# A two-layer graph network on one core: layer two's first block held by chunks of inputs, one block's rows moved in the DMA queue, and the last superblocks' weight sums read from PSUM

## The chip, the cores and the metric

The kernel runs on one core of a Trainium2 chip, in one launch. The metric is the device time of that launch in microseconds; three runs of the kernel before give its median. Beside the runs there is one profiled execution, from which all views of the trace come: PE (TensorE, the matmuls), PEld (its weight loads), DVE (VectorE), ACT (ScalarE), POOL (GpSimd) and SP (SyncE, which here only issues DMAs).

## What is computed

`x` is 128 × 64 × 768 (batches, positions, features), `adj` 128 × 64 × 64. All is float32. Cut to what matters:

```python
h = maximum(layernorm(x), 0)
for l in range(2):
    m_left  = einsum('bsh,oh->bso', h, W_left[l])
    m_right = einsum('bsh,oh->bso', h, W_right[l])
    u_left  = einsum('bih,bjh->bij', h, m_left) / sqrt(768)
    u_right = einsum('bih,bjh->bij', h, m_right) / sqrt(768)
    u = u_left on and above the diagonal of adj, u_right below it
    attention = exp(u) * adj, normalised over j
    h_lin = einsum('bsh,oh->bso', h, W_lin[l]) + b_lin[l]
    ctx = attention @ h_lin
    h = relu((ctx - mean) / (std + eps) * ln_a[l] + ln_b[l])
out = x + h
```

The two score products and the linear map are matrix products of 8192 tokens with 768 × 768 weights.

## The kernel before

**Parts, blocks, superblocks.** The 8192 tokens are 16 blocks of 512 (T), or 32 parts of 256 (TH), 4 batches each. `HT` holds a part's inputs transposed: features on the partitions, six chunks (C) of 128, as a tile `ht` of [128, 6, 256]. `SUPER` (L173) groups the parts that are worked on together: first the two parts (0, 1), then eleven superblocks of three parts.

**Pass one** (`pass_one`, L655) makes scores and attention. The products of tokens with W_left and W_right go by a fast bilinear scheme: three groups of tokens against blocks of 256 × 256 of the weights, in 40 products (`PRODUCTS`) instead of 54. Each product multiplies a signed sum of weight blocks (a "form", `W_OPS`) with a signed sum of token blocks (`T_OPS`, made by class `Tokens`, mostly on POOL); six of the 40 use a raw token block, index below 9. `product` (L691) issues eight matmul instructions of 256 columns (a float32 matmul appears as two instructions), the result lies in one of six PSUM banks (C, D, X, Y, Z, V, taken in turn), and `reads` (L904) adds it with its coefficients into the score operands M: the first touch of each by an ACT copy (L910), the others by DVE (L245, the helper `added`, and L914). A product must wait until its bank was read. Behind a superblock come its scores (L733) and softmax.

**The first block of layer two** is different. Layer two's k = 0 covers one block of 512 tokens. The three groups are thirds of each batch's 64 positions, 22 wide (`WIDE`, `THIRDS`, L579 to L581), so a product has 8 × 22 = 176 columns. The block lies in two `ht` tiles, one for each part (four batches, six chunks). A raw token block therefore is two pieces of 88 columns, one in each tile, and its product takes 16 instructions instead of 8; sums that read a raw block are made in two halves of 176 elements (`value(..., cut=True)`). Weight forms of layer two were made in layer one and lie in DRAM; 20 are fetched ahead (`forms_first`, L1328), the others during k = 0, each into a buffer that came free (`fetch`, L936 to L937 and in `turn_of`).

**Pass two** (`pass_two`, L1012) takes one block after another: h_lin (`linear`, L1226, 15 products of `ORDER`, L1006), context (L1048), and the normalisation in `finish` (L1182): squares (L1193) into a buffer `z` (a ring of four), then the scaled rows (L1211), which are stored (`kept`, L1180). In the last two blocks of layer one (u = 14 and 15) layer two is prepared: rows of blocks 0 and 1 are loaded (`load_rows`, L344, eight DMAs), transposed by DVE into `xb`, stored (L461, four DMAs), and loaded again transposed (`load_h`, L370, two DMAs of 768 KB), where the affine map and relu are applied by ACT (`affine`, L383, L379).

**What sets the order.** All is written out in program order. A product or multiplication i opens slots 2i and 2i + 1; `put(slot, f)` hangs a step on a slot, `run` issues it there, and each engine works through its own instructions in that order. All transfers here are issued by SP through one queue, in order: a DMA that waits holds those behind it. The lines around the change:

```python
1271  put(27, lambda: load_rows(1, 1, sp))           # in the loop, u = 14
1289  load_h(1, 1, 0)                                # start of u = 15
1290  put_all(24, transpose_rows(1, 1, sp), 2)
1293  put(48, lambda: load_h(1, 1, 1))
1294  put_all(28, affine(1, 1, 0), 3)
```

**The last superblock of each layer** also prepares the linear weights of pass two (`final_of`, L1310): they are loaded, centred by ACT with sums and differences (`centre`, L218, L233 and L237, slots 28 on), and 16 signed sums of them are made (`sums_n`, L247), the even ones on POOL, the odd ones on DVE, from slot 42 on, two in every three slots. `bias` (L955) treats the bias rows likewise; its `combined` (L978) adds three of them on DVE (L979, L980).

Of the kernel before, what the change touches and what calls it, by code (L numbers as in the profile page):

```python
# [17 lines left out]
def kernel(  # L18
# [12 lines left out]
    nc = tc.nc  # L31
# [549 lines left out]
    CUT = PB * WIDE  # L581

    class Tokens:
# [11 lines left out]
        def value(self, k, v, cut=False):  # L595
            if v >= 9:
                t = self.at[k, v]
                if k:
                    return [t]
                t = t[:, :, :2 * CUT]  # L600
                return [t[:, :, h * CUT:(h + 1) * CUT].rearrange("p c (b s) -> p c b s", b=PB)
                        for h in range(2)] if cut else [t]
            j = v // 3
            if k:
                return [HT[1, self.l, SUPER[k][v % 3]][:, j * K2:(j + 1) * K2, :]]
            r = THIRDS[v % 3][0]
            return [HT[1, self.l, p][:, j * K2:(j + 1) * K2, :].rearrange("p c (b s) -> p c b s", s=S)[:, :, :, r:r + WIDE]
                    for p in SUPER[0]]
# [7 lines left out]
        def emit(self, eng):  # L616
# [4 lines left out]
            cut = a < 9 or b < 9  # L621
            for o, x, y in zip(*(self.value(self.k, n, cut) for n in (v, a, b))):
# [12 lines left out]
        def need(self, k, v):  # L635
            while v >= 9 and (k, v) not in self.at:
                self.emit(nc.gpsimd)
            return self.value(k, v)
# [16 lines left out]
    def pass_one(l, start, final):  # L655
        with tc.tile_pool(name=f"one{l}", bufs=2, reuse_waits="tile") as sp, \
# [34 lines left out]
            def product(bank, w, ts, new, slot, n=TH):  # L691
                p = bank[:, :2 * n].rearrange("p (g n) -> p g n", g=2)
                for g in range(2):
                    for c in range(K2):
                        at = 0
                        for t in ts:
                            t = t[:, c]
                            n = math.prod(t.shape[1:])
                            o = p[:, g, at:at + n]
                            if len(t.shape) == 3:  # L700
                                o = o.rearrange("p (b s) -> p b s", b=t.shape[1])
                            nc.tensor.matmul(o, w[:, c, g * P:(g + 1) * P], t,  # L702
                                             start=(new and g == c == at == 0), stop=(c == K2 - 1),
                                             skip_group_check=True)
                            at += n
# [659 lines left out]
```

## Time and profile before

| | us |
|---|---|
| median of three runs | 2652.43 (2652.22 to 2653.41) |
| the profiled execution | 2648.42 |
| its span, first to last instruction | 2646.6 |
| PE busy | 2591.6 (98%) |
| DVE busy | 1780.6 (67%) |
| POOL busy | 1763.1 (67%) |
| ACT busy | 935.4 (35%) |

The mean granted TensorE clock was 0.995 of full speed. A line of the timeline gives start, duration, engine, source line, operation, what is written and read, and the count; in brackets stands the idle time of the engine before it and what ended it. In the lists of DMA issues the last number is the time from issue to landing. Where the profile names one releaser, an instruction may have waited for several things, of which it names the one that it saw last.

### The profile page before, as it was taken

How to read it: one execution, taken by the hardware profiler on the slowest of the kernel's cores; microseconds unless marked ns; L12 is line 12 of the kernel's file. 1: busy time of each engine (PE TensorE's matmuls, PEld its weight loads, DVE VectorE, ACT ScalarE, POOL GpSimd, SP SyncE). 2: the span in 40 equal slices, each digit the busy share in tenths (PEclk: the TensorE clock that was granted, in tenths of full speed). 3: DMA queues.
4: the chain of work that ended last, by engine and by line, in shares of the span. 5: the costliest groups of instructions: out<-in, count | busy, mean ns of one | idle time of the engine just before them, and what ended most of it. 6: DMA issues, size and time to landing. Idle time of an engine off the chain costs nothing. (4 is left out here: it accounts for less than half of the span.)

```text
span 2646.6 us, 47202 instructions
## 1 busy us (share of the span) xinstructions
PE 2591.6 (98%) x18122; PEld 2217.1 (84%) x18122; DVE 1780.6 (67%) x2888; ACT 935.4 (35%) x1969; POOL 1763.1 (67%) x1392
## 2 busy tenths in 40 slices
PE   9899999999999999999999999999999989999998
PEld 8788888888888888888798888888888878887886
DVE  7878787777768445554456667677666676666667
ACT  5522223223113244454542222122222335555453
POOL 4766676666668657676276666667666657878786
PEclk9999999999999999999999999999999999999999
DMA  7443534343421354445794424253532215555655
GB/s 220 113 111 86 124 93 110 93 119 79 98 60 56 123 156 149 159 139 182 219 282 101 121 68 108 71 129 93 136 98 70 67 49 157 157 167 166 177 161 146
DMA packets 258465, 331.84 MB, mean 125 GB/s; under 512 B 56002, under 2 KB 190402, under 8 KB 258242
## 3 DMA queue, kind: packets, MB, share of 16 engines
q1 hardware_dynamic: 241442, 320.56, 44.3%
q10 hardware_dynamic: 16800, 8.26, 1.2%
q8 instruction: 145, 2.38, 0.4%
q14 instruction: 78, 0.64, 0.1%
HBM read 213.39 MB, written 115.34 MB: 124 GB/s over the span
## 5 line engine op out<-in xcount | busy, mean ns | idle before, releaser
L245 POOL TENSOR_TENSOR g<-ht 128x512 f32<-128x512 f32 (+1 forms) x620 | 785.9, 1279 | 420.8 <-PE Z L702 71.6
L245 POOL TENSOR_TENSOR g<-g,g 128x512 f32<-128x512 f32 (+1 forms) x310 | 397.9, 1291 | 136.7 <-PE C L702 22.0
L245 POOL TENSOR_TENSOR g<-ht,g 128x512 f32<-128x512 f32 (+1 forms) x272 | 346.1, 1282 | 164.8 <-PE Z L702 42.8
L702 PE MATMUL X<-g,g 128*128 128x256 f32 (+1 forms) x1080 | 252.9, 377 | 6.0 <-DVE m L914 6.0
L1006 PE MATMUL Z<-g,g 128*128 128x256 f32 x1024 | 244.1, 380 | 3.5 <-ACT hl L300 3.2
L702 PE MATMUL C<-g,g 128*128 128x256 f32 x1008 | 239.7, 381 | 4.9 <-POOL g L245 2.2
L702 PEld LDWEIGHTS X<-g,g 128*128 128x128 f32 x1080 | 203.0, 191 | 34.8 <-DVE m L914 6.8
L702 PE MATMUL Y<-g,g 128*128 128x256 f32 (+1 forms) x968 | 225.7, 376 | 3.8 <-POOL g L245 3.8
L1006 PEld LDWEIGHTS Z<-g,g 128*128 128x128 f32 x1024 | 191.6, 190 | 35.8 <-issue 4.1
L379 ACT ACTIVATE ht<-ht,b_col,a_col 128x256 f32<-128x256 f32 x384 | 196.1, 591 | 69.0 <-DMA ht<-h 53.8
L702 PEld LDWEIGHTS C<-g,g 128*128 128x128 f32 x1008 | 190.5, 190 | 32.9 <-POOL g L245 3.5
L702 PE MATMUL Z<-g,g 128*128 128x256 f32 (+1 forms) x936 | 217.0, 375 | 0.0
L702 PE MATMUL D<-g,g 128*128 128x256 f32 x880 | 209.8, 381 | 1.8 <-POOL g L245 1.8
L702 PEld LDWEIGHTS Y<-g,g 128*128 128x128 f32 x968 | 182.0, 190 | 27.8 <-POOL g L245 4.2
L702 PE MATMUL V<-g,g 128*128 128x256 f32 (+1 forms) x840 | 194.6, 375 | 3.1 <-POOL g L245 1.6
L702 PEld LDWEIGHTS Z<-g,g 128*128 128x128 f32 x936 | 174.5, 190 | 23.1
L702 PEld LDWEIGHTS D<-g,g 128*128 128x128 f32 x880 | 168.1, 191 | 25.7 <-POOL g L245 2.5
L1006 PE MATMUL X<-g,g 128*128 128x256 f32 x768 | 182.7, 379 | 0.0
L702 PEld LDWEIGHTS V<-g,g 128*128 128x128 f32 x840 | 157.6, 191 | 23.3 <-POOL g L245 1.7
L1206 POOL TENSOR_TENSOR z<-z,b 128x768 f32<-128x768 f32 x62 | 112.7, 1829 | 81.7 <-DVE z L1203 77.2
L245 DVE TENSOR_TENSOR m<-m,Y 128x512 f32<-128x512 f32 (+2 forms) x196 | 126.5, 667 | 58.4 <-ACT m L910 35.7
L245 DVE TENSOR_TENSOR m<-m,D 128x512 f32<-128x512 f32 x180 | 118.2, 677 | 70.0 <-ACT m L910 51.3
(222 smaller groups left out, 4612.0 us busy)
## 6 DMA issues: line engine op xcount, KB each, us to landing
ht<-h SPq DMA_DIRECT2D x126, 768.0 KB, 6.3
h<-xb SPq DMA_DIRECT2D x124, 384.0 KB, 6.6
z<-z SPq DMA_DIRECT2D x128, 192.0 KB, 3.1
x<-z SPq DMA_DIRECT2D x128, 192.0 KB, 5.4
xr<-in_x_dram SPq DMA_DIRECT2D x120, 192.0 KB, 3.8
out_dram<-xr SPq DMA_DIRECT2D x120, 192.0 KB, 2.7
x<-in_x_dram SPq DMA_DIRECT2D x112, 192.0 KB, 5.4
g<-form SPq DMA_DIRECT2D x40, 256.0 KB, 5.6
```

The costliest lines, as they stand in the source:

```text
L245: (eng.tensor_add if sign == "+" else eng.tensor_sub)(o, a, b)
L379: nc.scalar.activation(ht, ht, AF.Relu, bias=cols[1][:, c:c + 1], scale=cols[0][:, c:c + 1])
L702: nc.tensor.matmul(o, w[:, c, g * P:(g + 1) * P], t, start=(new and g == c == at == 0), stop=(c == K2 - 1), skip_group_check=True)
L1006: nc.tensor.matmul(p[:, n], b[t][:, c, r * P:(r + 1) * P], w[s][:, c, :], start=(i in FIRST and i not in PRELOAD and n == c == 0), stop=(c ...
L1206: nc.gpsimd.tensor_add(zs[k], zs[k], rows["b"])
```

## The change

It has three parts.

1. **First block of layer two.** Its 512 tokens are held as two `ht` tiles of three chunks and all tokens, instead of two of six chunks and half the tokens. `load_both` fills them by four DMAs of 384 KB (pieces of 1 KB in each partition) in place of two of 768 KB. A raw token block lies in one tile, or, for the middle pair of chunks, one chunk in each. Raw products take eight instructions of 176 columns instead of 16 of 88. Token sums that read raw blocks are one operation of 352 elements, save where a middle block is read: these stay two, by chunk. The affine map takes six ACT operations of 512 elements instead of twelve of 256.
2. **Second block of layer two.** Its row loads move from slot 27 of u = 14 to slot 1 of u = 15, behind the first block's loads; the transposes from slots 24 to 36 to slots 32 to 44 and their store from 40 to 48; the loads of the transposed block from slot 48 to 54, behind the stores of z from u = 15's first half (slots 51 and 52).
3. **Last superblock of each layer.** For the eight odd sums, and for both additions in `combined`, ACT first copies one operand into PSUM (bank Z or V in turn), and DVE reads it there.

The diff, cut to its core:

```diff
@@ sums_n
-            added((nc.gpsimd, nc.vector)[n % 2], t[o], s, t[a], t[b])
+            x = t[a]
+            if n % 2:
+                x = KEEP["ZV"[n // 2 % 2]].rearrange("p (c d) -> p c d", c=K2)
+                nc.scalar.copy(x, t[a])
+            added((nc.gpsimd, nc.vector)[n % 2], t[o], s, x, t[b])
...
+    CUT = 2 * PB * WIDE
+
+    def load_both(l):
+        for n in range(2):
+            t = HT[1, l, n] = big.tile([P, C, TH], F32, name="ht", bufs=6).rearrange("p c t -> p (c t)").rearrange(
+                "p (c t) -> p c t", t=T)
+            for p in range(2):
+                nc.sync.dma_start(t[:, :, p * TH:(p + 1) * TH], KEPT[l][p][:, n * C // 2:(n + 1) * C // 2])
+
+    def both_of(l, c, n):
+        return HT[1, l, 2 * c // C][:, c % (C // 2):c % (C // 2) + n]
+
+    def affine_both(l):
+        def part(c):
+            t = both_of(l, c, 1)[:, 0]
+            nc.scalar.activation(t, t, AF.Relu, bias=cols[1][:, c:c + 1], scale=cols[0][:, c:c + 1])
+
+        return [lambda c=c: part(c) for c in range(C)]
...
@@ Tokens.emit
-            cut = a < 9 or b < 9
-            for o, x, y in zip(*(self.value(self.k, n, cut) for n in (v, a, b))):
+            if self.k == 0 and (a // 3 == 1 or b // 3 == 1):
+                for c in range(K2):
+                    added(eng, *([self.value(0, v, c), sign] + [self.value(0, n, c) for n in (a, b)]))
+            else:
+                o, x, y = (self.value(self.k, n) for n in (v, a, b))
...
                 added(eng, o, sign, x, y)
@@ product
-                        at = 0
-                        for t in ts:
-                            t = t[:, c]
-                            n = math.prod(t.shape[1:])
-                            o = p[:, g, at:at + n]
...
+                        t = tok(c)
+                        o = p[:, g] if len(t.shape) == 2 else p[:, g].rearrange("p (b s) -> p b s", s=WIDE)
+                        nc.tensor.matmul(o, w[:, c, g * P:(g + 1) * P], t, start=(new and g == c == 0),
+                                         stop=(c == K2 - 1), skip_group_check=True)
@@ combined
-            nc.vector.tensor_add(t[1], t[1], t[0])
-            nc.vector.tensor_add(t[3], t[1], t[2])
+            a, b = (KEEP[n][:, :D] for n in "ZV")
+            nc.scalar.copy(a, t[0])
+            nc.scalar.copy(b, t[2])
+            nc.vector.tensor_add(t[1], t[1], a)
+            nc.vector.tensor_add(t[3], t[1], b)
@@ pass_two, u = 14
-                        put(27, lambda: load_rows(1, 1, sp))
@@ pass_two, u = 15
-                        load_h(1, 1, 0)
-                        put_all(24, transpose_rows(1, 1, sp), 2)
+                        load_both(1)
+                        put(1, lambda: load_rows(1, 1, sp))
+                        put(31, lambda: put_all(32, transpose_rows(1, 1, sp), 2))
                         put_all(2, [fetch.popleft() for _ in range(8)], 2)
                         put_all(46, [lambda: TOKENS[1].step(0)] * Tokens.LIMIT, 1)
-                        put(48, lambda: load_h(1, 1, 1))
-                        put_all(28, affine(1, 1, 0), 3)
+                        put(54, lambda: load_h(1, 1, 1))
+                        put_all(28, affine_both(1), 3)
```

More of the change, by code (lines that the diff above doesn't have):

```diff
@@ L592, in __init__, with value @@
             self.count = {}
-        def value(self, k, v, cut=False):
+        def value(self, k, v, c=None):
+            if k:
+                t = self.at[k, v] if v >= 9 else HT[1, self.l, SUPER[k][v % 3]][:, v // 3 * K2:(v // 3 + 1) * K2, :]
+                return t if c is None else t[:, c, :]
             if v >= 9:
[L597 to L608, printed above, removed]
+                t = self.at[k, v][:, :, :CUT]
+                return t if c is None else t[:, c].rearrange("p (b s) -> p b s", s=WIDE)
+            n, r = v // 3 * K2 + (c or 0), THIRDS[v % 3][0]
+            t = both_of(self.l, n, K2 if c is None else 1).rearrange("p c (b s) -> p c b s", s=S)[:, :, :, r:r + WIDE]
+            return t if c is None else t[:, 0]
         def step(self, slot, eng=None):
@@ L689, in pass_one, with product @@
                 "p (k h) -> p k h", k=2) for g in range(2)]
-            def product(bank, w, ts, new, slot, n=TH):
+            def product(bank, w, tok, new, slot, n=TH):
                 p = bank[:, :2 * n].rearrange("p (g n) -> p g n", g=2)
@@ L729, in scores @@
                             b = q % 2 * PAIR + h
-                            mb = both[:, c, q // 2 * PB + b] if l and k == 0 else m[:, c, b]
+                            if l and k == 0:
+                                b += q // 2 * PB
+                                hc, mb = both_of(l, c, 1)[:, 0], both[:, c, b]
+                            else:
+                                hc, mb = ht[:, c], m[:, c, b]
                             mb = mb.rearrange("p k j -> p (k j)")
@@ L882, in pass_one @@
                     tok = HT[1, l, t][:, j * K2:(j + 1) * K2, :]
-                    product(bank, weights.at[3 * w + j], [tok], j == 0, slot)
+                    product(bank, weights.at[3 * w + j], lambda c, tok=tok: tok[:, c, :], j == 0, slot)
                     weights.used(3 * w + j)
@@ L919, in pass_one @@
                     w, tok = weights.need(f), tokens.need(k, t)
-                    product(bank_of(CHAINS * (k - 1) + i % CHAINS), w, tok, i < CHAINS, slot, TH if k else 2 * CUT)
+                    product(bank_of(CHAINS * (k - 1) + i % CHAINS), w, tok, i < CHAINS, slot, TH if k else CUT)
                     tokens.used(k, t)
```

15 lines of the change are left out of this document (5 added, 10 removed).

## The prediction

> **What bounds the kernel now.** I read the page first, its share of each engine, then the busy time by stretches, and then the timeline of the stretches that the diff touches.
>
> ```profile
> PE 2591.6 (98%) x18122; PEld 2217.1 (84%) x18122; DVE 1780.6 (67%) x2888; ACT 935.4 (35%) x1969; POOL 1763.1 (67%) x1392
> 820.00:864.00 44.00, 39.20 (x300) 33.08 (x299) 38.79 (x57) 12.19 (x38) 34.62 (x27) 1.00 0.04 11
> 1297.00:1336.00 39.00, 35.87 (x189) 25.02 (x188) 15.40 (x36) 24.68 (x56) 8.04 (x16) 1.00 1.00 307
> 1336.00:1392.50 56.50, 53.44 (x369) 52.84 (x368) 31.67 (x66) 22.37 (x49) 40.92 (x60) 0.97 0.93 271
> 1392.50:2088.00 695.50, 690.74 (x5672) 609.05 (x5674) 477.62 (x779) 171.44 (x331) 460.71 (x368) 1.00 0.39 96
> ```
>
> The page gives TensorE 98% of the span, so time is won only by fewer or shorter matmuls, or where PE waits. The stretches (columns: length, then PE, weight loads, DVE, ACT, POOL, then clock, DMA share, GB/s) show where that is: 820 to 864 is layer one's last superblock, with DVE at 38.8 of 44; 1297 to 1336 is the last block of layer one's second pass and 1336 to 1392.5 is layer two's first block, and in both the DMA engines are all but full (1.00 and 0.93). Behind that, from 1392.5 on, PE works 690.7 of 695.5: little there can hand back or swallow what happens ahead of it.
>
> PE's waits in these stretches, from the timeline (start, duration, idle before and its releaser):
>
> ```profile
> 837.23 1.99 PE L702 MATMUL X<-g,g 128*128 128x256 f32 x8 [2.90 <-DVE m L914]
> 848.62 1.97 PE L702 MATMUL C<-g,g 128*128 128x256 f32 x8 [0.58 <-DVE m L245]
> 1317.60 1.13 PE L1006 MATMUL Z<-g,g 128*128 128x256 f32 x4 [1.68 <-ACT hl L300]
> 1320.41 1.13 PE L1006 MATMUL Z<-g,ht 128*128 128x256 f32 x4 [0.81 <-ACT hl L300]
> 1327.06 1.13 PE L1006 MATMUL Z<-g,ht 128*128 128x256 f32 x4 [0.47 <-ACT hl L300]
> 1391.15 1.43 PE L702 MATMUL V<-g,g 128*128 128x176 f32 x8 [1.47 <-DVE m L914]
> 2137.22 3.38 PE L702 MATMUL X<-g,g 128*128 128x256 f32 x8 [3.10 <-DVE m L914]
> ```
>
> The profiled execution took 2648.42 us, of which 1.8 lie outside its span of 2646.6. The median of the three runs is 2652.43, 4.0 above it. I make the sum as a difference in the profiled execution and add it to the median.
>
> **Part one, layer two's first block.** Its six products of raw tokens lose half their matmuls.
>
> ```profile
> 1359.47 1.36 PE L702 MATMUL X<-g,g 128*128 128x176 f32 x8
> 1360.66 1.91 PE L702 MATMUL Y<-ht,g 128*128 128x88 f32 x16
> 1362.41 1.39 PE L702 MATMUL Z<-g,g 128*128 128x176 f32 x8
> 1384.90 0.36 SPq L651 DMA_DIRECT2D g<-form  x1
> g<-form SPq DMA_DIRECT2D x1, 256.0 KB, 6.1
> ```
>
> From start to start a raw product (16 instructions of 88) costs 1362.41 − 1360.66 = 1.75 us, a summed one (8 of 176) 1360.66 − 1359.47 = 1.19. Six products save 6 × 0.56 = 3.4 us of PE. But the last product of this block, at 1391.15, needs the last weight form, which SP issues at 1384.90 and which lands 6.1 us later (the last row, an answer on DMA issues at that moment): at 1391.0. The DVE that the profile names is not what came last. So a PE that arrives 3.4 us earlier waits 3.4 us longer, unless the form comes earlier too. **The DMA queue decides here**, and it is one queue in order, nearly full: the form comes earlier only by what is gained or lost in gaps of the transfers ahead of it.
>
> ```profile
> 1334.52 0.93 SPq L368 DMA_DIRECT2D ht<-h  x1
> ht<-h SPq DMA_DIRECT2D x1, 768.0 KB, 6.6
> 1345.33 0.60 ACT L379 ACTIVATE ht<-ht,b_col,a_col 128x256 f32<-128x256 f32 x1 [1.11 <-DMA ht<-h]
> DMA packets 344, 1.08 MB, mean 362 GB/s; under 512 B 59, under 2 KB 59, under 8 KB 344
> DMA packets 3050, 2.94 MB, mean 367 GB/s; under 512 B 180, under 2 KB 3050, under 8 KB 3050
> 1294.54 1.99 SPq L461 DMA_DIRECT2D h<-xb  x1
> h<-xb SPq DMA_DIRECT2D x1, 384.0 KB, 7.9
> ```
>
> - A gap that goes. Today the second load of the other block waits for a store: the first load lands at 1334.52 + 6.6 = 1341.1, the second at 1345.3 (ACT starts on it then). 768 KB at 362 GB/s (the row of 1342 to 1345 us) is 2.2 us, so 4.2 − 2.2 = 2.0 us are empty. In the new order four z stores (192 KB each, 2.2 us by the same rate) stand ahead of these loads and fill the gap: −1.9.
> - A gap that comes. The new loads go to the head of the last block, and the second needs the last transposed store, which lands at 1294.54 + 7.9 = 1302.4. Today rows stream behind that store without a break. A load needs about 2 us from its issue to its first bytes, by the empty 2.0 just found, and the first quarter (384 KB, 1.1 us at 367 GB/s) needs only an earlier store and covers part: +0.8.
> - The pieces. 4 loads of 384 KB in 1-KB pieces replace 2 of 768 KB. The row with 3050 packets (8 to 16 us: weights in 1-KB pieces, 256 KB each) shows 367 GB/s: 4 × 1.07 = 4.3 against 2 × 2.2 = 4.4 us: −0.1. The Trainium skill (DMA: Bandwidth & Descriptors, Rules for kernel authors) speaks against this edit: it asks for 1 MiB or more in a DMA. By that the halved loads would move slower and the form would land later; the two rows, 362 and 367 GB/s, do not bear it out.
>
> Sum for the form: −1.9 + 0.8 − 0.1 = −1.2, ends −2.1 (no new gap) and +1.2 (the old gap not filled, a new one of 1.2). The PE needs 3.4 and gets 1.2.
>
> The token sums and the affine step are cheaper, and I cost them at nothing:
>
> ```profile
> L245 POOL TENSOR_TENSOR g<-ht 128x176 f32<-128x176 f32 x33 | 16.6, 535 | 0.0
> L245 POOL TENSOR_TENSOR g<-g,g 128x352 f32<-128x352 f32 x12 | 11.2, 937 | 0.5
> ```
>
> Two sums of 176 (2 × 0.54, or about 1.0 pitch to pitch) become one of 352 (0.94): about 0.1 each, under 2 us in all, on an engine busy 40.9 of 56.5. Without this cover the loss is at most the same 2 us.
>
> **Part two, the second block's rows behind the stores.** What SP does now at the end of layer one, and why ACT holds PE there:
>
> ```profile
> 1296.57 6.88 SPq L361 DMA_DIRECT2D x<-z  x8
> 1306.90 1.19 SPq L1180 DMA_DIRECT2D z<-z  x2
> z<-z SPq DMA_DIRECT2D x2, 192.0 KB, 7.6
> 1315.07 0.81 ACT L1193 ACTIVATE z<-aux 128x768 f32<-128x768 f32 x1 [2.73 <-PE Z L1006]
> 1324.53 0.81 ACT L1193 ACTIVATE z<-aux 128x768 f32<-128x768 f32 x1 [0.25 <-DMA z<-z]
> ```
>
> The squares at 1315.07 write a z buffer that the stores of 1306.90 must first empty; they land 7.6 us later, at about 1315.0. PE had long been done. ACT stands 2.73 us, and PE's evictions stand behind it: 1.68 + 0.81 = 2.5 us of the waits listed. Those stores are late because eight row loads (6.9 us) went ahead. With the rows behind, the stores land some 5 us earlier (6.9 less the new gap and the loads' pieces) and this wait goes: −2.5. What is late next: the squares at 1324.53, which today wait 0.25 for the next z stores. Ahead of those the queue carries as much as before, the rows now among it, plus the new gap of 0.8: they land 0.8 later, while PE and ACT get there 2.5 earlier. So ACT stands there instead, and the wait before 1327.06 (0.47) grows by about 2.7. Net +0.2, between −2.5 (nothing late) and +0.8. It hardly matters for the end, since the form at 1391 is set by the queue: what PE gains here it waits for there.
>
> The four transposes move by 8 slots with their store (40 to 48), and the second block's loads by 6 (48 to 54), past the z stores. SP waits for the store before the second load, as today; behind it on SP stand z stores and the next rows, which the full queue would hold anyway. I cost this at nothing; what it costs without that cover is the slower rival.
>
> **Part three, the staged weight sums.** Per layer eight copies of 512 and two of 256 come onto ACT; DVE's sums read PSUM.
>
> ```profile
> L245 DVE TENSOR_TENSOR g<-g,g 128x512 f32<-128x512 f32 x8 | 10.0, 1246 | 0.0
> L245 DVE TENSOR_TENSOR m<-m,Y 128x512 f32<-128x512 f32 x11 | 7.0, 675 | 0.0
> L979 DVE TENSOR_TENSOR g<-g 128x256 f32<-128x256 f32 x1 | 1.5, 1480 | 0.0
> L980 DVE TENSOR_TENSOR g<-g,g 128x256 f32<-128x256 f32 x1 | 1.4, 1369 | 0.0
> 821.15 0.68 DVE L245 TENSOR_TENSOR g<-g,g 128x512 f32<-128x512 f32 x1
> 824.65 0.40 ACT L233 ACTIVATE g<-g 128x256 f32<-128x256 f32 x1
> 825.57 0.16 DVE L228 TENSOR_REDUCE wmm<-wm 128x2 f32<-128x6 f32 x1 [1.66 <-ACT g L233]
> 831.39 0.69 DVE L245 TENSOR_TENSOR m<-m,D 128x512 f32<-128x512 f32 x1 [1.17 <-ACT m L910]
> 851.12 0.59 ACT L995 COPY Z<-g 128x512 f32<-128x512 f32 x1
> ```
>
> With PSUM as one operand a sum of 512 takes 0.675, so eight go from 10.0 to 5.4; L979 and L980, of 256, from 2.9 to at most 1.35 (two at the price of 512): DVE is relieved of 4.6 + 1.5 = 6.1 us a layer. The Trainium skill (SBUF — State Buffer, Who interferes with whom) says why: a DVE instruction with two SBUF inputs contends with a GpSimd one that reads SBUF, one with a single SBUF input doesn't. The rows agree (1.25 in the mean against 0.675).
>
> But the copies queue on ACT behind the centring of the weights, in slot order. DVE reaches the first odd sum at 821.15; the copy for it (slot 43) stands just ahead of the centring step of slot 44, which ACT starts at 824.65. With 0.59 for the copy (the last row) DVE gets its operand at 825.3, 4.1 us late. Of that, 1.66 and 1.17 us are waits that DVE has today (at 825.57 and 831.39), but the first one's release comes from ACT, whose next steps wait for DVE's L229 in turn, so that ACT falls back by about 2 and by another 1.2 for two more copies. At 831.39 DVE is then about 2.7 late. From there to the wait at 837.23 one sum and L979, L980 give back about 1.1 + 1.5 = 2.6, and the next copies (0.59 and two smaller) hold it up by some 0.2. So PE's wait of 2.90 stays as it is: +0.3, ends −1.2 and +1.35. Behind it the last sums give DVE 2 us more, which takes at most the 0.58 at 848.62, in layer one alone. I take −0.3 for layer one and +0.3 for layer two: 0.0 in all, ends −2.5 and +2.7.
>
> **The sum:** −1.2 (form) + 0.0 (last superblocks) = −1.2: 2647.2 for the profiled execution, 2651.2 beside the median.
>
> **Rivals.**
> - **DVE's relief arrives.** If the copies come in time (ACT runs ahead of its slots), 6.1 us a layer cover the waits at 837.23 and 848.62 and at 2137.22: 2.90 + 0.58 + 3.10 = 6.6 us, 2644.6 with the form's −1.2. For: DVE is the engine named at all three, ACT is busy only 12.2 of 44. Against: 824.65 behind 821.15. It decides whether the first copies run more than 2 us earlier than I have them. The port rule of the skill's page is on this side.
> - **Slower: the second block's store comes late.** Transposes and store start 8 slots later, four products of layer one's last linear, about 1.1 us each by the row of 1327.06 (1.13): 4.3 us or so. If the queue doesn't run late enough to hide that, the loads behind the store land 4.3 us later than 1345.3, ACT stands in its in-order affine steps, first touches queue behind them, and all later transfers up to the form move too: +4.3, 2656.7. It decides where the new store, once issued, finds the queue empty. Against: the queue is full there (1.00), so the store has its turn behind older transfers in any case. With the last superblocks' upper end (+2.7) it is 2659.4.
> - **The change doesn't do what it says for PE:** the form stays where it is because the old gap isn't filled: 2652.4, inside the forecast's range.
>
> **How the numbers follow.** About 0.2%, 5.3 us, is what a measurement of this kernel can tell from no change. Forecast and unfilled gap together 0.47, own range 2648.5 to 2654.5; relief arrives 0.32, of which nearly all is faster by over 0.2% (below 2647.1); late store 0.21, about two thirds of it beyond 2657.7. So faster 0.31, same 0.55, slower 0.14. The range reaches over the relief (to 2643.0, room for a wait or two more) and up to 2657.0.
>
> **What would show it.** Raw products at 1.19 us. The last product of the first block still waiting, 2 us or more, its form landing about 1.2 earlier: right; no wait and the form long there: wrong. The 2.73 before the squares gone, another before the squares of the next half. DVE waiting about 4 us for the first copy, and PE's wait near 837 still about 3 us: if that wait is gone, my ACT order was wrong and the time is near 2644. A wait on the load at 1345 grown to several us would be the slower rival.

## The result, and the profile after

The changed kernel takes 2655.61 us in the median of 17 runs (2651.14 to 2660.46), the kernel before 2652.03 in 17 runs on the same chips (2648.43 to 2653.43). The ratio is 1.0017 with a 95% interval of 1.0011 to 1.0023: about 4.5 us **slower** (2.9 to 6.1) by that ratio, 3.6 between the medians, where 1.2 faster was forecast. The time lies inside the outer range (up to 2657.0), above the range of the forecast's own sum (2648.5 to 2654.5), and on the other side of no change.

The profiled execution took 2658.36 us (span 2656.6), 2.8 above its median, while that of before lay 3.6 under its own. So the two profiles differ by 10 us, and not all of that belongs to the change: at the end of layer one's scores, 868.79 us in the one and 872.68 in the other, 3.9 us are gone already, in stages that the change leaves alone for nearly all their length. Positions of the two traces are compared below after these 3.9 us.

The page's line of busy times, and the busy time by stretches of the changed kernel (length, PE, weight loads, DVE, ACT, POOL, granted clock, DMA share, GB/s). The second and third stretch are layer one's last linear and layer two's first block:

```profile
PE 2587.9 (97%) x18074; PEld 2214.7 (83%) x18074; DVE 1768.8 (67%) x2888; ACT 943.0 (35%) x1983; POOL 1755.0 (66%) x1377
824.00:868.00 44.00, 38.82 (x285) 32.22 (x287) 33.35 (x57) 16.27 (x45) 32.04 (x27) 1.00 0.04 11
1300.00:1345.60 45.60, 37.30 (x191) 27.09 (x189) 15.84 (x39) 22.82 (x48) 9.32 (x13) 0.93 0.96 278
1345.60:1402.00 56.40, 50.97 (x325) 50.07 (x325) 33.06 (x70) 22.80 (x50) 38.59 (x48) 0.96 0.88 262
1335.50:1339.20 3.70, 3.63 (x9) 2.92 (x10) 0.75 (x2) 1.30 (x4) 2.90 (x5) 0.50 0.91 239
1398.00:1404.00 6.00, 5.78 (x16) 5.15 (x17) 3.46 (x9) 0.00 (x0) 1.98 (x2) 0.50 0.00 0
```

PE has 48 instructions and 3.7 us less, as the wide matmuls promise, and the span is longer: PE waits more. In the last two rows it works at half its clock. The waits of PE in the timeline:

```profile
832.42 2.00 PE L719 MATMUL X<-g,g 128*128 128x256 f32 x8 [1.37 <-DVE wmm L229]
835.34 1.97 PE L719 MATMUL Y<-g,g 128*128 128x256 f32 x8 [0.92 <-DVE m L245]
840.57 1.99 PE L719 MATMUL D<-ht,g 128*128 128x256 f32 x8 [1.54 <-DVE m L245]
...
1335.57 2.08 PE L1028 MATMUL Z<-g,ht 128*128 128x256 f32 x4 [7.77 <-ACT hl L304]
1337.44 1.92 PE L1028 MATMUL Y<-g,ht 128*128 128x256 f32 x4
1339.15 1.12 PE L1028 MATMUL Z<-g,g 128*128 128x256 f32 x4
...
1398.22 2.68 PE L719 MATMUL V<-g,g 128*128 128x176 f32 x8 [3.55 <-DMA g<-form]
```

The waits of 1.68 and 0.81 us ahead of the third and the fifth product of the last linear's second half are gone. At its ninth product, where 0.47 stood, PE now waits 7.77 us; that product takes 2.08 us and the next 1.92 instead of 1.1: the clock is down. At the end of the first block the last form holds PE 3.55 us instead of 1.47, and the next 6 us run at half clock. What ACT does at the first of these, and SP's issues and their landings around it:

```profile
1315.27 0.81 ACT L1215 ACTIVATE z<-aux 128x768 f32<-128x768 f32 x1 [1.02 <-DMA x<-z]
...
1329.30 0.81 ACT L1215 ACTIVATE z<-aux 128x768 f32<-128x768 f32 x1 [4.87 <-DMA z<-z]
1330.01 0.19 ACT L1215 ACTIVATION_READ_ACCUMULATOR z<-aux 128x1 f32 x1
1333.32 0.81 ACT L1215 ACTIVATE z<-aux 128x768 f32<-128x768 f32 x1 [3.12 <-DMA z<-z]
```

```profile
1304.72 2.87 SPq L592 DMA_DIRECT2D ht<-h  x4
1307.63 1.39 SPq L1202 DMA_DIRECT2D z<-z  x2
1309.06 6.93 SPq L365 DMA_DIRECT2D x<-z  x8
...
1326.88 1.10 SPq L1202 DMA_DIRECT2D z<-z  x2
...
1341.15 4.67 SPq L1202 DMA_DIRECT2D z<-z  x4
z<-z SPq DMA_DIRECT2D x2, 192.0 KB, 5.8
```

The squares (L1215 here, L1193 before) no longer wait 2.73 us at 1315; they wait 4.87 + 3.12 = 8.0 us at 1329 and 1333, for the stores of the next two z buffers. The second buffer's were issued at 1326.88 and landed 5.8 us later (the last row), at 1332.7. Before, they were issued at 1320.07 and landed 3.8 us later, at 1323.9, or 1327.8 with the 3.9 us: they come **4.9 us later**, not 0.8.

### The profile page after: what moved, and what is told of

Read it like the earlier page. It is cut to its first block, busy times and chain, and to the rows that moved or that the text cites. A ratio compares the mean times of both kernels' runs of the same rounds, so it can differ in the third digit from the quotient of the medians.

```text
span 2656.6 us, 47106 instructions
## 1 busy us (share of the span) xinstructions
PE 2587.9 (97%) x18074; PEld 2214.7 (83%) x18074; DVE 1768.8 (67%) x2888; ACT 943.0 (35%) x1983; POOL 1755.0 (66%) x1377
## 5 line engine op out<-in xcount | busy, mean ns | idle before, releaser
L245 POOL TENSOR_TENSOR g<-ht 128x512 f32<-128x512 f32 (+2 forms) x611 | 781.9, 1290 | 429.5 <-PE X L719 82.7
L245 POOL TENSOR_TENSOR g<-ht,g 128x512 f32<-128x512 f32 (+2 forms) x266 | 345.0, 1305 | 165.1 <-PE Z L719 42.4
L383 ACT ACTIVATE ht<-ht,b_col,a_col 128x256 f32<-128x256 f32 x372 | 189.7, 591 | 66.6 <-DMA ht<-h 44.7
L245 DVE TENSOR_TENSOR hl<-hl,Z 128x512 f32<-128x512 f32 (+1 forms) x136 | 83.1, 652 | 123.6 <-PE Z L1028 121.7
```

The source lines that it names most:

```text
L245: (eng.tensor_add if sign == "+" else eng.tensor_sub)(o, a, b)
L383: nc.scalar.activation(ht, ht, AF.Relu, bias=cols[1][:, c:c + 1], scale=cols[0][:, c:c + 1])
```

## The experiments

Each run of five rounds stands beside runs of the kernel before on the same chip; the ratio is to those, with its 95% interval. The stages are read from PE's timeline of each profile: A from the first linear product behind layer one's scores (868.79 before) to the context product in the last linear's second half (1321.51); B from there to the last context product of layer one (1333.62); C from there to the first product behind the first block's scores (1404.68).

| run | ratio to before | A | B | C | A+B+C |
|---|---|---|---|---|---|
| before | | 452.7 | 12.1 | 71.1 | 535.9 |
| before, second profile | | 452.5 | 12.2 | 73.5 | 538.2 |
| changed | 1.0017 (1.0011 to 1.0023) | 450.4 | 20.6 | 71.5 | 542.5 |
| changed, second profile | | 451.0 | 18.9 | 69.9 | 539.9 |
| part one alone | 1.0012 (1.0003 to 1.0020) | 452.1 | 13.0 | 72.7 | 537.8 |
| part two alone | 1.0003 (0.9994 to 1.0012) | 450.6 | 18.5 | 72.7 | 541.8 |
| part two alone, second profile | | 450.6 | 19.4 | 66.7 | 536.7 |
| part three alone | 1.0006 (0.9997 to 1.0015) | 453.1 | 13.2 | 71.6 | 538.0 |
| changed without part two | 1.0002 (0.9993 to 1.0010) | 452.4 | 13.5 | 71.9 | 537.9 |
| changed, z stores first | 1.0022 (1.0013 to 1.0031) | 455.2 | 13.3 | 71.4 | 539.8 |
| changed, six z buffers | 1.0014 (1.0005 to 1.0024) | 450.9 | 11.2 | 79.5 | 541.5 |
| changed, form first | 1.0001 (0.9991 to 1.0011) | 451.6 | 18.6 | 64.3 | 534.4 |
| changed, buffers and form | 0.9994 (0.9985 to 1.0002) | 450.0 | 11.4 | 72.9 | 534.4 |
| the same, affine later | 0.9994 (0.9985 to 1.0003) | 450.0 | 11.4 | 73.4 | 534.8 |
| parts one and three, buffers and form | 0.9984 (0.9975 to 0.9993) | 450.0 | 11.4 | 70.5 | 531.9 |
| part one, buffers and form | 0.9984 (0.9975 to 0.9992) | 450.0 | 11.4 | 69.7 | 531.1 |
| the same, waiting steps later | 0.9993 (0.9984 to 1.0002) | 450.0 | 11.4 | 72.9 | 534.3 |
| before, buffers and form | 0.9989 (0.9980 to 0.9998) | 450.6 | 11.8 | 72.0 | 534.4 |

Three profiles with the old rows and the old first block (the two of before and part three alone) give A 452.8, B 12.5, C 72.1 in the mean; the two of the changed kernel 450.7, 19.7 and 70.7. That is −2.1, +7.2 and −1.4: +3.8 us in all, which is the result within its interval. The sum scatters by some 2 us between profiles of one kernel, in part two alone by 5.

**The theory after the first look** was that part two had put the z stores behind the rows and loads, so that ACT, and PE behind it, stood there. **The rival**: that the loads of part one, which landed slowly in the changed kernel's profile, cost the time. First the parts alone.

### Part one alone

```diff
-                        load_h(1, 1, 0)
+                        load_both(1)
...
-                        put_all(28, affine(1, 1, 0), 3)
+                        put_all(28, affine_both(1), 3)
```

> Part one alone on the kernel before: the block held by chunks, the four smaller loads, the wide matmuls; rows, transposes and sums stay where they were. Theory (the loss comes from part two, where the z stores of block 14 queue behind the rows and hold ACT): between 2 us faster and 1 us slower than before, with the wait ahead of the ninth product of the last linear under 2 us. Rival (the loads in 1-KB pieces, which took about 1.7 us each in the changed kernel's profile, 7 us for four, cost the time): slower than before by 3 to 5 us, with most of the long wait of 7.8 us already there.

Measured: 2654.04 us, ratio 1.0012 (1.0003 to 1.0020), 1 to 5 us slower. The middle, 3.2 us, is outside the theory's bounds (at most 1 slower) and inside the rival's (3 to 5), the interval allows both. What tells them apart is the trace: the rival's long wait isn't there (1.59 us ahead of the third product of the last linear's second half and 1.31 ahead of the ninth, against 1.68 and 0.47 before), and A to C take what they take in the old kernel. The saving of 3.4 us in the six products doesn't appear: the last product of the first block now waits longer for its form (4.16 us). So part one by itself gains nothing, and the slow pieces by themselves don't make the stage B of the changed kernel.

### Part two alone

```diff
-                        put(27, lambda: load_rows(1, 1, sp))
...
-                        put_all(24, transpose_rows(1, 1, sp), 2)
+                        put(1, lambda: load_rows(1, 1, sp))
+                        put(31, lambda: put_all(32, transpose_rows(1, 1, sp), 2))
...
-                        put(48, lambda: load_h(1, 1, 1))
+                        put(54, lambda: load_h(1, 1, 1))
```

> Part two alone on the kernel before: rows of the second block in slot 1 of the last block, transposes, store and loads later; the first block still loaded by two DMAs of 768 KB. Theory (rows ahead of the z stores): slower than before by 2 to 6 us, with a wait of 4 to 7 us ahead of the ninth product of the last linear and a granted clock near 0.5 behind it. Rival (pieces): within 1.5 us of before, the wait there under 2.5 us.

Measured: 2654.27 us, ratio 1.0003 (0.9994 to 1.0012). The wait is there as the theory has it, the loss of 2 to 6 us is not. A second profile asks whether the wait comes in every execution:

> Part two alone, unchanged, for a second profile. Theory: a wait of 4 to 7 us ahead of the ninth product. Rival (it comes in some executions only, which would explain why the timed runs show next to no loss): under 2.5 us there.

Its time was 2650.32 us. PE's timeline, first in the first profile, then in the second:

```profile
1336.53 2.08 PE L1006 MATMUL Z<-g,ht 128*128 128x256 f32 x4 [5.58 <-ACT hl L300]
1338.40 1.68 PE L1006 MATMUL Y<-g,ht 128*128 128x256 f32 x4
```

```profile
1330.72 2.08 PE L1006 MATMUL Z<-g,ht 128*128 128x256 f32 x4 [5.20 <-ACT hl L300]
1332.59 1.91 PE L1006 MATMUL Y<-g,ht 128*128 128x256 f32 x4
...
1391.80 1.39 PE L702 MATMUL Z<-g,g 128*128 128x176 f32 x8
1393.03 1.36 PE L702 MATMUL V<-g,g 128*128 128x176 f32 x8
```

The wait of over 5 us, with the half clock behind it, is in both. But in the second profile the last product of the first block starts without a wait: a PE that is late doesn't wait for the form. C falls to 66.7 there. So a part of what stage B loses can be given back at the form, in this execution 5 of 7 us, which fits the timed runs' small loss. In the changed kernel, whose wide matmuls save PE 3.4 us ahead of the same form, PE waits there in both profiles (3.55 and 3.14 us).

### Part three alone

The edit is part three of the diff, on the kernel before.

> Part three alone on the kernel before: the odd weight sums and the bias sums read one operand from PSUM. Both theories: within 1.5 us of before. If the relief of DVE arrives after all, 4 us or more faster; if the copies hold DVE up, 2 us or more slower.

Measured: 2653.44 us, ratio 1.0006 (0.9997 to 1.0015): no difference, and none in the last superblocks' length. The changed kernel's DVE and ACT show why:

```profile
824.18 0.69 DVE L245 TENSOR_TENSOR m<-m,D 128x512 f32<-128x512 f32 x1 [0.85 <-PE D L719]
829.05 0.69 DVE L245 TENSOR_TENSOR g<-Z,g 128x512 f32<-128x512 f32 x1 [4.18 <-ACT Z L256]
...
833.90 0.69 DVE L245 TENSOR_TENSOR g<-V,g 128x512 f32<-128x512 f32 x1 [1.52 <-ACT V L256]
...
837.88 0.69 DVE L245 TENSOR_TENSOR g<-Z,g 128x512 f32<-128x512 f32 x1 [1.89 <-ACT Z L256]
```

Each sum takes 0.69 us now, so the relief is there; but DVE stands 4.18, 1.52 and 1.89 us for the first three copies (L256), which ACT reaches late. PE's one wait of 2.90 has become three of 1.37, 0.92 and 1.54.

### The z stores ahead of the rows

```diff
-                        put(1, lambda: load_rows(1, 1, sp))
+                        put(17, lambda: load_rows(1, 1, sp))
...
-                        put_all(2, [fetch.popleft() for _ in range(8)], 2)
+                        put_all(18, [fetch.popleft() for _ in range(8)], 2)
```

> The changed kernel with the second block's rows in slot 17 instead of 1, and the eight forms behind them (slots 18 to 32), so that the z stores of block 14 (slots 14 and 16) go ahead of both. Theory: the wait of 7.8 us ahead of the ninth product falls to 1 us or less and the clock stays at 1.0 there; 5 to 9 us faster than the changed kernel, 1 to 5 us faster than the kernel before. Rival (pieces): the wait stays above 4 us, since the slow loads still stand ahead, and the time stays within 2 us of the changed kernel's.

Measured: 2658.69 us, ratio 1.0022 (1.0013 to 1.0031): no gain on the changed kernel. The theory's wait went, and its time didn't come: the wait moved. DVE's first transpose now stands for the rows, and ACT's scaling for DVE:

```profile
1325.02 0.98 DVE L469 STREAM_TRANSPOSE xb<-x 128x768 f32<-128x768 f32 x1 [6.80 <-DMA x<-z]
```

```profile
1326.62 1.69 ACT L1233 ACTIVATE z<-aux,rs 128x768 f32<-128x768 f32 x2 [5.04 <-DVE rs L1221]
```

Behind the transpose in DVE's order stands the reciprocal (L1221) for which ACT waits, and PE stood 5.09 us ahead of the context product. The experiment was meant to free one wait; in neither of the two orders do rows and z stores both come in time, with the steps at these slots.

### Six z buffers; the changed kernel without part two; the form first; both

```diff
-                            "xb": ([P, H // 32, Q, 32], 1), "z": ([P, H], 4)}, ("hl", "at", "x", "xb", "z"))
+                            "xb": ([P, H // 32, Q, 32], 1), "z": ([P, H], 6)}, ("hl", "at", "x", "xb", "z"))
...
-                zs = [sp.tile([P, H], F32, name="z", bufs=4) for _ in range(2)]
+                zs = [sp.tile([P, H], F32, name="z", bufs=6) for _ in range(2)]
```

> The changed kernel with six z buffers instead of four, so that the squares needn't wait for the stores of the block before. Theory (part two's loss is this wait of ACT on late z stores): no wait over 1 us ahead of the ninth product of the last linear, the clock 1.0 there, and the first block of layer two starts 8 to 9 us earlier than in the changed kernel's profile. But the last weight form of that block comes when the queue brings it, so its wait grows by 3 to 6 us: net 2 to 5 us faster than the changed kernel, within 2 us of the kernel before. Rival (the wait is a matter of slow loads and their own waits): the wait stays above 4 us and the time within 1 us of the changed kernel's.

Measured: 2658.69 us, ratio 1.0014 (1.0005 to 1.0024). Stage B falls from 20.6 to 11.2 us, the shortest of all runs: the wait on the z stores was the whole of its excess. And C rises to 79.5. PE and ACT in that profile:

```profile
1345.49 1.36 PE L719 MATMUL X<-g,g 128*128 128x176 f32 x8
1354.22 2.69 PE L719 MATMUL Y<-g,g 128*128 128x176 f32 x8 [7.37 <-issue]
```

```profile
1349.89 0.60 ACT L383 ACTIVATE ht<-ht,b_col,a_col 128x256 f32<-128x256 f32 x1 [5.77 <-DMA ht<-h]
1353.18 0.60 ACT L383 ACTIVATE ht<-ht,b_col,a_col 128x256 f32<-128x256 f32 x1 [2.69 <-DMA ht<-h]
1353.68 0.43 ACT L929 ACTIVATE m<-Y 128x336 f32<-128x336 f32 x1
```

That is the mechanism of the prediction's slower rival, in its place: ACT stands in its in-order affine steps for the second block's loads, the first touch (L929) behind them frees the bank, and PE waits 7.4 us. The wait that the buffers took away had only hidden it. And the last product of the block starts 524.8 us behind the start of A, where the changed kernel's two profiles have 525.5 and 524.1, although nothing stood for the z stores: the last form comes as late without that wait as with it.

> The changed kernel without part two: first block by chunks and staged sums, the second block's rows, transposes and loads in their old slots. Theory: no long wait in the last linear (under 2.5 us each), the form's wait at the end of the first block 3 to 5 us instead of 1.6; 0 to 3 us slower than the kernel before, 1 to 4 us faster than the changed kernel. Rival (the parts cost nothing together but noise): within 1 us of the changed kernel.

(The edit is part two of the diff, undone.) Measured: 2655.50 us, ratio 1.0002 (0.9993 to 1.0010), waits of about 2 us each in the last linear, the form's wait 4 us. Against 1.0017 with part two: beside the other two parts, part two costs about 4 us (alone it cost 1, −2 to 3), and the others cost nothing that the runs can tell.

```diff
-                    put(end + (8 if b == 2 else 0), lambda: load_rows(l, b + 1, sp))
+                    put(end + (10 if b == 2 else 0), lambda: load_rows(l, b + 1, sp))
```

> The changed kernel with the row loads of block 3 put one slot later, so that the last weight form of layer two's first block goes ahead of them in the queue. Theory (the form's place in the queue takes back what the wide matmuls save, and the clock falls to 0.5 after the wait): the wait of 3.55 us ahead of the last product and the slow 6 us behind it go; the first block takes 65 to 67 us from its first product to the second group's after the scores, instead of 71.5; 4 to 6 us faster than the changed kernel. Rival (the DVE sums named by the profile hold that product): the wait stays, within 1 us of the changed kernel.

Measured: 2655.60 us beside 2654.69 for before, ratio 1.0001 (0.9991 to 1.0011), some 4 us below the changed kernel's ratio. One DMA is moved ahead of eight, and C falls to 64.3 us, while the wait at the ninth product is still there (4.58 us, B 18.6):

```profile
1394.58 1.36 PE L719 MATMUL Z<-g,g 128*128 128x176 f32 x8
1395.77 1.36 PE L719 MATMUL V<-g,g 128*128 128x176 f32 x8
1396.97 1.89 PE L719 MATMUL C<-g,g 128*128 128x256 f32 x8
```

No wait ahead of the last product, and full clock behind it. That the form holds this product in the old kernel too, where the first profile named DVE, is what the second profile of before says itself:

> The kernel before, unchanged, for a second profile. Theory: the last linear of layer one and the first block as in the first profile within 2 us, the other stages up to 4 us longer, since the first profile was of an execution 4 us under the median.

```profile
1393.21 1.61 PE L702 MATMUL V<-g,g 128*128 128x176 f32 x8 [3.16 <-DMA g<-form]
1394.61 3.44 PE L702 MATMUL C<-g,g 128*128 128x256 f32 x8
```

(Its time was 2651.09 us.) The second profile of the changed kernel, 2658.14 us, has the two waits again: 6.24 us at the ninth product and 3.14 for the form.

> The changed kernel, unchanged, for a second profile. Theory (the wait on the z stores is in each execution): a wait of 4 to 8 us ahead of the ninth product of the last linear, the form's wait of 3 to 4 us. Rival (it comes in some executions only): under 2 us there.

Both mends together:

> Both: six z buffers and the last form ahead of block 3's rows. Theory: both waits gone, 9 to 13 us faster than the changed kernel and 5 to 9 us faster than the kernel before. Rival (a third wait, on the loads of the second block or on POOL's token sums, takes their place): less than 5 us faster than the changed kernel.

Measured: 2653.06 us, ratio 0.9994 (0.9985 to 1.0002): about 6 us below the changed kernel, between the theory's 9 to 13 and the rival's under 5. B is 11.4 us and the form's wait is gone; ACT's affine steps hold PE 6.3 us, the third wait that the rival had in view. Beside the form alone (1.0001) the buffers bring nothing that the intervals can tell; the profiles' sums are 534.4 both times.

### The steps that wait, put later

```diff
-                follow[1] = [24, 24]
-                put_all(10, affine(1, l, 1))
+                follow[1] = [44, 44]
+                put_all(30, affine(1, l, 1))
```

> The changed kernel with six z buffers, the last form ahead of block 3's rows, and the affine steps of the second block in slots 30 to 35 of layer two's first pass instead of 10 to 15. Theory (in the run with two of these mends ACT stood 5.0 and 2.4 us in that in-order step for the loads that part two makes late, and the first touches behind it held PE 6.3 us): that wait falls under 2 us and the first block takes 65 to 67 us instead of 72.9; 4 to 8 us faster than the run with two mends, 6 to 10 us faster than the kernel before. Rival (POOL's token sums or the DVE set that point too): the first block stays above 70 us and the time within 2 us of the run with two mends.

Measured: 2651.49 us, ratio 0.9994 (0.9985 to 1.0003), no better. ACT's wait went, and DVE stood in its own in-order step for the rows of block 2, with PE behind it (DVE, then PE):

```profile
1359.50 1.84 DVE L469 STREAM_TRANSPOSE xb<-x 128x768 f32<-128x768 f32 x2 [9.68 <-DMA x<-z]
```

```profile
1361.88 2.69 PE L719 MATMUL Z<-g,g 128*128 128x176 f32 x8 [7.83 <-DVE m L933]
```

The rival was right, with DVE's transpose as the point. Then the same two mends on the old row order, with parts one and three, with none of the change, and with part one alone:

> Parts one and three on the old order of the rows, with six z buffers and the last form ahead of block 3's rows. Theory: the waits of about 2 us each in the last linear go with the buffers, the form's wait with the form; 6 to 10 us faster than the kernel before. Rival (the second block's loads then hold ACT in its affine steps here too): a wait of 3 us or more in the first ten products, under 4 us faster.

> The kernel before with the same two mends and nothing of the change. Theory (the wide matmuls of part one are worth 3.4 us once the form no longer binds): 3 to 6 us faster than before, and 3 to 4 us slower than parts one and three with the mends. Rival (part one is worth nothing in any order): within 1 us of that run.

> Part one alone on the old order, with the two mends, without the staged sums. Theory (part three is worth nothing): within 1.5 us of the run with parts one and three. If the relief of DVE counts after all: 2 to 7 us slower than that run.

Measured: 2647.84 us, 0.9984 (0.9975 to 0.9993); 2649.42 us, 0.9989 (0.9980 to 0.9998); 2647.64 us, 0.9984 (0.9975 to 0.9992); before on that chip 2652.32. So the two mends alone are worth about 3 us, and part one on top of them another 1.6 to 1.8 by the medians (3 in the profiles' sums: 534.4 to 531.1 and 531.9), less than the 3 to 4 expected and not told from nothing by the intervals. Part three is worth nothing here either. **These two versions, part one with six z buffers and the form first, beat both kernels**: by the ratios by about 4 us the one before, by about 9 the changed one.

What was left in the one with part one alone was 3.3 us ahead of the tenth product, again ACT's affine steps (ACT stood 2.73 us there for the loads), and 1 us behind DVE's transposes. One more run put both later still (the steps that count from these slots move with them):

```diff
-                put_all(10, affine(1, l, 1))
+                put_all(20, affine(1, l, 1))
...
-    pass_one(1, {"weights": 3, "tokens": 0, 2: 18}, final_of(1))
+    pass_one(1, {"weights": 3, "tokens": 0, 2: 28}, final_of(1))
```

> Part one with six z buffers and the last form ahead of block 3's rows, on the old row order, and now also the in-order steps that wait for transfers set later in layer two's first pass: the affine steps of the second block in slots 20 to 25 instead of 10 to 15, the preparation of block 2 from slot 28 instead of 18. Theory (each in-order step that comes ahead of its transfer holds its engine, and with it the first touches): the waits of 3.4 and 1.0 us in the first block and the half clock behind them go, the first block takes 65 to 67 us instead of 69.7, 3 to 5 us faster than without, 7 to 10 us faster than the kernel before. Rival (the queue is late for everything, and the wait turns up at the next step): the first block stays at 69 us or more.

Measured: 2649.78 us, ratio 0.9993 (0.9984 to 1.0002), no better than without, and 3 us worse by the profiles' sums. The wait of 3.3 us went; at the block's end, where the next superblock's token sums and DVE's readings were now late, PE waited again:

```profile
1390.51 1.99 PE L715 MATMUL D<-g,g 128*128 128x256 f32 x8 [1.70 <-POOL g L245]
1394.64 3.65 PE L715 MATMUL X<-g,g 128*128 128x256 f32 x8 [2.14 <-DVE m L245]
```

## Why the prediction was wrong

**Right: the last superblocks.** 0.0 forecast; part three alone shows no difference. DVE's wait for the first copy was put at 4.1 us and is 4.18. PE's wait of 2.90 did not stay one wait: with the 0.58 behind it it became three, 3.83 in all against 3.48. The first rival, relief in full, is refuted.

**Right: who holds the last product.** The form, not DVE, ends the wait at the end of the first block; the six products save 3.4 us of PE (1.19 us each now); and PE waits there instead, 3.55 and 3.14 us. Moving one DMA ends the wait.

**Right: the first wait goes.** −2.5 forecast, stage A −2.1.

**Wrong: when the form comes.** The step that failed is the form's term, −1.9 + 0.8 − 0.1 = −1.2, which was the whole sum. The form was to land 1.2 us earlier, and the last product of the first block to start as much earlier. Counted from the start of A, that product starts at 525.5 and 524.1 us in the changed kernel's two profiles, against 522.4, 523.0 and 522.7 in the three with the old rows and the old first block: 2.1 us later. From there to the end of C it takes 1.7 us more, which fits the half clock behind the longer wait. Together that is the +3.8. (That stage C alone is 1.4 shorter, close to the forecast's −1.2, is chance: C begins 5.1 us later.)

It is the new order of part two that makes the form late. The product starts at 522.2 to 523.0 us in the five profiles that keep the old order and the form's old place, and at 523.2 to 528.3 in the six with part two and that place (in the lowest of them PE came after the form); without part two the loss is gone (1.0002), and so it is with the form moved ahead (1.0001).

The term of −1.9 had nothing to win. It took 2.0 of the 4.2 us between the landings of the second block's two loads, 1341.1 and 1345.3, for empty. The kernel before in that stretch:

```profile
1341.00:1342.00 1.00, 1.00 (x8) 1.00 (x7) 0.10 (x1) 1.00 (x4) 0.92 (x3) 1.00 0.86 252
1342.00:1345.00 3.00, 3.00 (x23) 3.00 (x22) 0.91 (x2) 2.19 (x4) 2.92 (x5) 1.00 0.97 362
```

The DMA engines were busy for 0.86 and 0.97 of it and moved 1.3 MB, of which the load is 0.8: some 0.2 us were empty, not 2.0. The time from one landing to the next went to other transfers too. (The 2 us that the forecast gives a load from its issue to its first bytes rest on the same stretch, so no row shows them.) The third rival had the form stay where it is; it comes later than that, and why, with the gap about as wide as forecast, stays open.

**Wrong too: what is late next.** The next z stores were to "land 0.8 later", so that the wait at the ninth product grows by about 2.7, "net +0.2". They land 4.9 us later (3.8 by the squares' start in the second profile), PE waits 7.77 us (6.24), and stage B costs +7.2. Place and mechanism were as predicted, the size was not. Of this size the runs show:

- The gap that the new loads open. I put it at 0.8 us. The DMA engines in the changed kernel around these loads, and below it the kernel before in two stretches:

```profile
1306.00:1308.00 2.00, 2.00 (x11) 1.72 (x10) 0.58 (x2) 1.31 (x5) 0.00 (x0) 1.00 0.86 244
1308.00:1310.00 2.00, 2.00 (x11) 1.79 (x10) 0.67 (x3) 0.81 (x3) 0.00 (x0) 1.00 0.94 250
1310.00:1312.00 2.00, 1.95 (x10) 1.40 (x9) 0.90 (x3) 1.74 (x3) 0.00 (x0) 1.00 0.75 211
```

```profile
1302.00:1306.00 4.00, 4.00 (x21) 3.48 (x20) 1.36 (x5) 2.13 (x8) 0.00 (x0) 1.00 1.03 236
1306.00:1312.00 6.00, 5.89 (x36) 3.86 (x35) 3.34 (x7) 2.78 (x5) 0.00 (x0) 1.00 1.02 350
```

  Shares of 0.86, 0.94 and 0.75 leave 0.9 us of the six empty, where the kernel before has none: the gap is about as I put it. The GB/s don't show a loss, since the kernel before, too, moves only 236 with its engines full. So some 4 of the 4.9 us are not this gap. The stores are issued 2.9 us later (1326.88 against 1320.07 + 3.9) and take 2.0 longer to land; which transfers that belongs to isn't in the landings.
- The order, not the pieces. The second squares start 455.7 and 455.6 us behind the start of A in the two profiles of before, 458.8 and 458.4 with part two alone, 460.6 and 459.5 in the changed kernel. So part two alone makes 2.9 of the 4.4 us. The other 1.5 are no more than the scatter: part three alone has 457.3.
- The clock. After 7.77 us of waiting PE ran at 0.50 for 3.7 us, which costs 1.8 more, and after the form's 3.55 for 6 us, 3 more. My sum had no term for it, although the old kernel's rows show it: the product behind the wait of 3.10 us in layer two took 3.38 instead of 1.9. The Trainium skill (TensorE: Matmul & The Clock Gate, What's actually happening) says that an idle window of about 3.4 us brings half rate, and that about as long a busy stretch ends it. The traces agree in the second, with 3.4 to 6 us at half clock, and only roughly in the first: the length of one wait doesn't decide. The wait of 2.90 us in layer one's last superblock kept the clock in the profile of before, and that of 3.10 lost it; in other executions of the same code it was the other way round (part two alone, second profile; before, second profile):

```profile
838.37 3.57 PE L702 MATMUL X<-g,g 128*128 128x256 f32 x8 [2.92 <-DVE m L914]
2139.99 1.99 PE L702 MATMUL X<-g,g 128*128 128x256 f32 x8 [3.10 <-DVE m L914]
```

  And in the run with the waiting steps later, waits of 1.70 and 2.14 us with one product between them were enough (the product behind took 3.65 us).

For the end this long wait counted little, as the prediction's sentence "it hardly matters for the end, since the form at 1391 is set by the queue" has it. Six z buffers take the wait away, and neither the form nor the time gets better (524.8 us, 1.0014); moving the form leaves it, and the loss is gone. Nor does ACT's standing hold the queue up much: SP was at the transposed stores until 1340.37 and issued the z stores that wait for ACT at 1341.15, 0.8 us later.

**The slower rival** priced the late second block at +4.3 us and gave it 0.21. Its mechanism is real: it is what holds PE 7.4 us as soon as the z stores don't. In the changed kernel itself the wait ahead of it is longer, and no such wait shows.

**The pieces of 1 KB** are not the cause of the long wait: part one alone has them and no long wait, part two alone has the wait (5.58 and 5.20 us) without them.

## What to carry to other kernels

When a wait is removed in a stage whose DMA queue is full, list every in-order step of every engine that stands on a transfer of that queue (here the squares on z stores, the transposes on rows, the affine steps on loads, the last product on its form), with its slack; removing one wait gives the next, and moving a block of transfers inside the queue pays one with the other. Before you count on a gap, read the DMA engines' share in it: the time between two landings is not empty because one transfer is shorter than it. Find the transfer that the end hangs on and move that, as one small urgent DMA ahead of eight unhurried ones did; two more buffers took the longest wait away and by themselves gained nothing. And a wait of PE of 2 to 3 us or more can have a second price, the half clock behind it.

## What the runs showed of the hardware

The waits of TensorE of 3.55 and 7.77 us were followed by 6 and 3.7 us at a granted clock of 0.50: products of 128x176 then took 2.7 us instead of 1.36 and those of 128x256 up to 3.6 instead of 1.9. Waits of about 3 us lost the clock in some executions and kept it in others (2.92 and 3.10 us above). Executions of one kernel differ by some us in the same stage (part two alone: C 72.7 and 66.7 us; A starts at 875.22 and at 869.80); with one profile of each I first read 10 us where the runs show 3.6 between their medians. And the releaser named at a wait can change between two executions of one kernel: the same product waits for "DVE m L914" in one profile of before and for "DMA g<-form" in the other.
